# Projecting a tile's attention output in two halves instead of four quarters

## The chip, the cores and the metric

The kernel runs on one core of one Trainium2 chip. The metric is the device time of one execution in microseconds, as the median of several runs. In the texts below TensorE, VectorE, ScalarE, GpSimd and SyncE are the core's engines; the profile calls them PE (with PEld for its weight loads), DVE, ACT, POOL and SP.

## What is computed

The program is a graph network of 1250 nodes with 512 features: two graph layers and two feed-forward layers that contain attention, each added to a running sum `x`. Only the last of them, the second attention, is touched by the change:

```python
qkv = x @ qkv_w.T + qkv_b                       # x here: normalised x plus a 3-wide convolution
q, k, v = jnp.split(qkv, [c, 2 * c], axis=-1)   # 8 heads of 64
logits = jnp.einsum('bmd,bpd->bmp', qd * scale, kd)
_, idx = lax.top_k(logits, 16)                  # each query keeps its 16 best keys
...
attn = jax.nn.softmax(jnp.einsum('bmd,bmkd->bmk', q * scale, k_sel), axis=-1)
out = jnp.einsum('bmk,bmkd->bmd', attn, v_sel)
...
return out @ wo_w.T + wo_b                      # the projection that the change re-cuts
```

The result of this layer is added to `x`, and that sum is the program's output, 1250 rows by 512 columns in float32.

## The kernel before, in words

The 1250 nodes are cut into 10 tiles of 125 rows. The second attention takes 40 steps in an order that is written out by hand (`tc.manual_schedule()`): each engine executes its instructions in the order in which the program emits them. Step `n` treats tile `n // 4` and one pair of heads, `c = n % 4`; the two heads of a pair are called 0 and 1. A step does the following.

- `scores1` (L1595): TensorE multiplies the queries of the tile with all 1250 keys into one of two score buffers, which take three PSUM banks each, one for each head of a pair. The score pair `scores1(n + 1, 0, 0)`, two matmuls, is the first work of the next step and stands in the middle of the emitted order.
- `largest1`, `first1`, `second1` (L1602 to L1626): VectorE finds each row's 16 largest scores and from them `nm`, the negated maximum, and `below`, the threshold.
- `weights1` (L1632): ScalarE writes the exponentials `e`. `select1` (L1639, L1642): ScalarE writes the signs `sg` of score minus threshold, the last read of a score buffer, and GpSimd multiplies `e` by them.
- `turn1(n - 1, g)` (L1652) and `keep1(n - 1, g)` (L1659): TensorE transposes the weights of the step before in five groups of four blocks, and ScalarE copies each group to `pT`, with a Relu that drops what was not selected.
- `values1(n - 2, ...)` (L1708) and `outputs1` (L1718): TensorE multiplies the transposed weights with the values of the step before that one, and ScalarE keeps the result in `oT`, for which three buffers are there.
- Once in a tile, spread over its four steps: the sums of the exponentials (L1668 to L1693), their transposes on TensorE (L1689) at c = 2, the scaling of `oT` (L1696) on GpSimd, and `halves1` (L1580 to L1583) for the next tile's queries.
- `project1(i - 1, c)` (L1726): with `i = n // 4 - 1`, TensorE multiplies the scaled `oT` of the tile two before the current one with 128 of the 512 columns of `w_o`, as a sum of four products. Each float32 product is two instructions in the profile. `finish1` (L1734, L1736): VectorE adds `X` to it in the tile `y1`, and after the last columns of a tile SyncE writes that to the output.

The groups of transposes, the sums of values, the transposed sums and the results of `project1` all live in one pool of two PSUM banks, `ps_to1`; each new tile of that pool gets a bank when the kernel is built, and waits until the tile that had the bank before has been read.

The condition `i >= 1` leaves the first eight steps without a projection. The 32 calls in the loop serve tiles 0 to 7; tiles 8 and 9 are projected in full width behind the loop, into the score buffers.

Of the kernel before, what the change touches and what calls it, by code (L numbers as in the profile page):

```python
# [22 lines left out]
D = 512  # L23
# [549 lines left out]
def tile_usual(ctx: ExitStack, tc: tile.TileContext, a: dict, out: bass.AP):  # L573
# [165 lines left out]
    with (  # L739
# [83 lines left out]
        for r in range(rounds):  # L823
# [7 lines left out]
            while order and (order[0][0] <= r or r == rounds - 1):  # L831
                _, i, t = order.pop(0)
# [720 lines left out]
    with (  # L1553
# [17 lines left out]
        def halves1(i, a_):  # L1571
            if i >= T:
                return
            if a_ == 0:
                stacks[i] = at1.tile([128, 2, H, P], F32R, name="stacks")
            S = stacks[i]
            own, other = PAIRS[a_]
            hi, lo = S[own, 0, a_::2, :], S[own, 1, a_::2, :]
            q = qT[own, :, span(i, i + 1)]
            nc.scalar.copy(hi, q)  # L1580
            nc.gpsimd.tensor_sub(lo, q, hi.bitcast(F32))
            nc.sync.dma_start(S[other, 1, a_::2, :].bitcast(F32), hi.bitcast(F32))
            nc.sync.dma_start(S[other, 0, a_::2, :].bitcast(F32), lo.bitcast(F32))  # L1583

        def scores1(n, a_, *chunks):
            if n > last:
                return
            i, j = steps[n]
            h = 2 * j + a_
            if (n, a_) not in score:  # L1590
                score[n, a_] = ps_s1[a_].tile([P, 3 * 512], F32, name="S")
            for c in chunks:
                n0, n1 = PIECES[a_][c]
                for x in range(2):
                    nc.tensor.matmul(score[n, a_][:, n0:n1], stacks[i][:, x, h, :], K2[:, h, n0:n1],  # L1595
                                     start=(x == 0), stop=(x == 1))


        def largest1(n, a_):
            largest[n, a_] = at1.tile([P, SEARCHED, 8], F32, tag=f"largest{a_}", name="largest")  # L1600
            for k in range(SEARCHED):
                nc.vector.max(out=largest[n, a_][:, k, :], in_=score[n, a_][:, k:N:SEARCHED])  # L1602
# [32 lines left out]
        def select1(n, a_):  # L1635
            if not 0 <= n <= last:
                return
            sg = at1.tile([P, N], F16, tag=f"sg{a_}", name="sg", bufs=1)
            nc.scalar.activation(sg, score.pop((n, a_))[:, :N], AF.Sign, bias=belows.pop((n, a_)),  # L1639
                                 accum_out=signs[:, 2 * n + a_ : 2 * n + a_ + 1])  # L1640
            e = es[n, a_]
            (nc.vector if 2 * n + a_ == 2 * last + 1 else nc.gpsimd).tensor_mul(e, e, sg)  # L1642
# [27 lines left out]
        def sums_exp1(i):  # L1670
            nc.scalar.activation(sums[i], sums[i], AF.Exp)
# [23 lines left out]
        def scale1(i):  # L1695
            nc.gpsimd.tensor_mul(oTs[i], oTs[i], sums.pop(i))  # L1696

        def values1(n, t0, t1):
            if not 0 <= n <= last:
                return  # L1700
            i, j = steps[n]
            if t0 == 0:
                outs[n] = ps_to1.tile([128, 512], F32, tag="to", name="O")
            pT = pTs[n]
            for t in range(t0, t1):
                for a_ in range(2):
                    h = 2 * j + a_
                    nc.tensor.matmul(outs[n][a_ * DH : (a_ + 1) * DH, :P],  # L1708
                                     V[:, t, h * DH : (h + 1) * DH], pT[:, a_ * T + t, :],
                                     start=(t == 0), stop=(t == T - 1))  # L1710
# [9 lines left out]
        def project1(i, c, width=D // K, y=None):  # L1720

            if y is None:
                y = ps_to1.tile([128, 512], F32, tag="to", name="O")[:P, :width]
            cols = slice(c * width, (c + 1) * width)
            for k in range(K):
                nc.tensor.matmul(y, oTs[i][:, k, :], w_o[:, k, cols], start=(k == 0), stop=(k == K - 1))  # L1726
            projected.append((i, cols, y))
# [16 lines left out]
        def keep_late1():  # L1744
            if lates:
                t, ps = lates.pop(0)
                nc.vector.tensor_add(V[:, t, :], ps[:P], v_b)
# [17 lines left out]
        with tc.manual_schedule():  # L1765
            nc.sync.dma_start(w_v, a["qkv"][:, 2 * D :].rearrange("(k p) f -> p k f", p=128))
            nc.sync.dma_start(v_b, bass.AP(tensor=a["v_b"].tensor, offset=a["v_b"].offset, ap=[[0, P], [1, D]]))
            for a_ in range(2):
                halves1(0, a_)
            scores1(0, 0, 0, 2, 1)  # L1770
            for n in range(len(steps)):


                i, c = n // K - 1, n % K
                if i >= 0 and c == 3:
                    scale1(i)
                select1(n - 1, 1)
                largest1(n, 0)
                values1(n - 2, 0, 5)
                first1(n, 0)  # L1780
                if n == 1:
                    keep_late1()
                second1(n, 0)
                values1(n - 2, 5, 8)
                turn1(n - 1, 0)
                keep1(n - 1, 0)
                values1(n - 2, 8, T)
                scores1(n, 1, 1)
                scores1(n, 1, 0)
                outputs1(n - 2)  # L1790
                if i >= 0 and c == 1:
                    sums_over1(i)
                weights1(n, 0)
                if i >= 0 and c == 2:
                    sums_turn1(i)
                    sums_keep1(i)
                turn1(n - 1, 1)
                scores1(n, 1, 2)
                if n < 2:
                    values_late1(T - 3 + 2 * n)  # L1800
                keep1(n - 1, 1)
                turn1(n - 1, 2)
                if i >= 0 and c == 0:
                    sums1(i)
                if i >= 1:
                    project1(i - 1, c)
                select1(n, 0)
                largest1(n, 1)
                keep1(n - 1, 2)
                finish1()  # L1810
                if c < 2:
                    halves1(steps[n][0] + 1, c)
                if i >= 0 and c == 1:
                    sums_wide1(i)
                scores1(n + 1, 0, 0)
                if i >= 0 and c == 0:
                    sums_exp1(i)
                if n == 1:
                    keep_late1()
                turn1(n - 1, 3)  # L1820
                keep1(n - 1, 3)
                first1(n, 1)
                if n == 0:
                    keep_late1()
                scores1(n + 1, 0, 2)
                scores1(n + 1, 0, 1)
                if n == 0:
                    values_late1(T - 2)
                weights1(n, 1)
                turn1(n - 1, 4)  # L1830
                keep1(n - 1, 4)
                second1(n, 1)

            n, i = len(steps), T - 1
            sums1(i)
            values1(n - 2, 0, 5)
            select1(n - 1, 1)
            turn1(n - 1, 0)  # L1840
            values1(n - 2, 5, T)
            keep1(n - 1, 0)
            outputs1(n - 2)
            sums_exp1(i)
            turn1(n - 1, 1)
            keep1(n - 1, 1)
            sums_over1(i)
            sums_wide1(i)
            y0 = ps_s1a.tile([P, 3 * 512], F32, name="S")
            y1 = ps_s1b.tile([P, 3 * 512], F32, name="S")  # L1850
            project1(i - 1, 0, D, y0[:, :D])
            turn1(n - 1, 2)
            keep1(n - 1, 2)
            finish1()
            sums_turn1(i)
            sums_keep1(i)
            turn1(n - 1, 3)
            keep1(n - 1, 3)
            R = sums.pop(i)
            oT = oTs[i]  # L1860
            nc.vector.tensor_mul(oT[:, : K - 1, :], oT[:, : K - 1, :], R[:, : K - 1, :])  # L1861

            def terms(*ks):
                for k in ks:
                    nc.tensor.matmul(y1[:, :D], oT[:, k, :], w_o[:, k, :], start=(k == 0), stop=(k == K - 1))  # L1865

            terms(0)
            turn1(n - 1, 4)
            signs_over1()
            terms(1)  # L1870
            keep1(n - 1, 4)
            values1(n - 1, 0, T)
            terms(2)
            nc.vector.tensor_mul(oT[:, K - 1, :], outs.pop(n - 1)[:, :P], R[:, K - 1, :])
            terms(K - 1)
            projected.append((i, slice(0, D), y1[:, :D]))
            finish1()
# [62 lines left out]
```

## Time and profile before

| what | value |
| --- | --- |
| median of 3 runs | 1506.62 us (1504.06 to 1507.05) |
| the profiled execution's own time | 1506.82 us |
| its span, first to last instruction | 1504.9 us |
| mean granted TensorE clock | 0.990 |
| second attention, 1110.07 to 1496.60 us | 386.53 us: TensorE busy 373.04, ScalarE 337.05, VectorE 299.97, GpSimd 244.64 |
| matmul instructions of `project1` in the loop (L1726) | 256 of 125 x 128, median 0.273 us |
| additions in `finish1` in the loop (L1734) | 32 of 125 x 128, median 0.269 us |

All times within the profile are microseconds from the start of the span. A busy TensorE in it is not TensorE at its peak, since matmuls are pipelined and their ends are modelled. A line such as L1726 is a line of the kernel. The idle time in square brackets is the engine's idle time ahead of a group of instructions, with the engine, tile and line that ended it.

### The profile page before, as it was taken

How to read it: one execution, taken by the hardware profiler on the slowest of the kernel's cores; microseconds unless marked ns; L12 is line 12 of the kernel's file. 1: busy time of each engine (PE TensorE's matmuls, PEld its weight loads, DVE VectorE, ACT ScalarE, POOL GpSimd, SP SyncE). 2: the span in 40 equal slices, each digit the busy share in tenths (PEclk: the TensorE clock that was granted, in tenths of full speed). 3: DMA queues.
4: the chain of work that ended last, by engine and by line, in shares of the span. 5: the costliest groups of instructions: out<-in, count | busy, mean ns of one | idle time of the engine just before them, and what ended most of it. 6: DMA issues, size and time to landing. Idle time of an engine off the chain costs nothing. (4 is left out here: it accounts for less than half of the span.)

```text
span 1504.9 us, 22522 instructions
## 1 busy us (share of the span) xinstructions
PE 1424.8 (95%) x8127; PEld 936.5 (62%) x8127; DVE 830.4 (55%) x2852; ACT 707.8 (47%) x1351; POOL 350.1 (23%) x301
## 2 busy tenths in 40 slices
PE   6999999978999998999999999998988999999997
PEld 4566744457778776544544445664447788888885
DVE  8995667644444332341111263565377888887774
ACT  2334434455555553301111122432148999999984
POOL 0110000011111111000000021320026666666662
PEclk9999999989999999999999999999999999999999
DMA  4001000010101000201000000000020001001000
GB/s 141 30 0 57 1 0 1 1 47 16 43 15 49 21 24 18 63 28 56 29 28 28 28 29 29 0 29 0 5 79 15 15 22 25 22 23 25 22 9 24
DMA packets 42332, 41.19 MB, mean 27 GB/s; under 512 B 25738, under 2 KB 30084, under 8 KB 42211
## 3 DMA queue, kind: packets, MB, share of 16 engines
q1 hardware_dynamic: 42211, 39.66, 9.0%
q8 instruction: 66, 1.08, 0.3%
q14 instruction: 55, 0.45, 0.1%
HBM read 26.81 MB, written 2.56 MB: 20 GB/s over the span
## 5 line engine op out<-in xcount | busy, mean ns | idle before, releaser
L1642 POOL TENSOR_TENSOR e<-e,sg 125x1250 f32<-125x1250 f32 x79 | 203.5, 2575 | 127.0 <-ACT sg L1639 75.0
L1602 DVE MAX8 largest<-S 125x8 f32<-125x89 f32 (+1 forms) x1120 | 183.9, 241 | 51.3 <-PE S L1595 51.2
L1336 DVE SCALAR_TENSOR_TENSOR X<-ps_o,gate,X 125x512 f32<-125x512 f32 x80 | 60.0, 749 | 177.1 <-PE ps_o L1334 177.1
L1595 PE MATMUL S<-K,stacks 128*125 128x512 f32 x480 | 133.5, 389 | 14.3 <-ACT sg L1639 6.2
L1334 PE MATMUL ps_o<-we,hid 128*125 128x512 f32 x320 | 141.2, 595 | 0.0
L1659 ACT ACTIVATE pT<-ps_t 125x500 f32<-125x500 f32 x200 | 117.8, 589 | 37.7 <-PE ps_t L1652 32.7
L1652 PE MATMUL ps_t<-ident,e 125*125 125x125 f32 x800 | 132.2, 285 | 2.8 <-ACT pT L1659 1.3
L1652 PEld LDWEIGHTS ps_t<-ident,e 125*125 125x125 f32 x800 | 109.5, 187 | 35.1 <-ACT pT L1659 14.3
L1329 ACT ACTIVATE hid<-ps_mm,b 128x500 f32<-128x500 f32 (+1 forms) x40 | 24.6, 615 | 209.0 <-PE ps_mm L1326 209.0
L1326 PE MATMUL ps_mm<-yT,we 128*128 128x500 f32 (+1 forms) x320 | 115.8, 520 | 0.0
L1708 PE MATMUL O<-pT,yT 125*64 125x125 f32 x1600 | 104.7, 275 | 0.2 <-ACT pT L1659 0.2
L1632 ACT ACTIVATE e<-S,nm 125x1250 f32<-125x1250 f32 x80 | 104.4, 1305 | 0.2
L1639 ACT ACTIVATE sg<-S,below 125x1250 f16<-125x1250 f32 x80 | 104.5, 1307 | 0.0
L1334 PEld LDWEIGHTS ps_o<-we,hid 128*125 128x125 f32 x320 | 59.0, 187 | 72.4 <-issue 69.6
L1127 ACT COPY pT<-ps_t 125x500 f32<-125x500 f32 (+3 forms) x112 | 54.8, 489 | 94.3 <-PE ps_t L1122 93.3
L1326 PEld LDWEIGHTS ps_mm<-yT,we 128*128 128x128 f32 x320 | 60.3, 189 | 55.2 <-issue 53.3
L1595 PEld LDWEIGHTS S<-K,stacks 128*125 128x125 f32 x480 | 72.7, 190 | 33.8 <-ACT sg L1639 18.0
L1708 PEld LDWEIGHTS O<-pT,yT 125*64 125x64 f32 x1600 | 85.8, 136 | 10.5 <-DVE bad L1762 0.8
L1034 PE MATMUL S<-K,stacks 128*125 128x512 f32 (+10 forms) x288 | 84.3, 401 | 7.1 <-ACT e L1101 6.6
L1122 PE MATMUL ps_t<-ident,e 125*125 125x125 f32 x440 | 81.7, 296 | 9.5 <-ACT pT L1127 6.0
L640 ACT ACTIVATE rs<-rs 125x1 f32<-125x1 f32 x60 | 12.1, 203 | 162.9 <-DVE rs L639 159.5
L1005 POOL TENSOR_TENSOR stacks<-yT,stacks 64x125 fp32r<-64x125 f32 x80 | 34.3, 428 | 232.1 <-ACT stacks L1004 229.0
(241 smaller groups left out, 2534.6 us busy)
## 6 DMA issues: line engine op xcount, KB each, us to landing
we<-in_W SPq DMA_DIRECT2D x16, 512.0 KB
stacks<-stacks SPq DMA_DIRECT2D x160, 31.2 KB
stacks<-stacks SPq DMA_DIRECT2D x40, 125.0 KB
X<-in_x SPq DMA_DIRECT2D x5, 500.0 KB
out<-y SPq DMA_DIRECT2D x10, 250.0 KB
w_n<-in_wn SPq DMA_DIRECT2D x1, 1024.0 KB
w_c<-in_wc SPq DMA_DIRECT2D x1, 1024.0 KB
w_q<-in_Wq SPq DMA_DIRECT2D x1, 1024.0 KB
```

Source lines behind the costliest of these rows:

```text
L1034: nc.tensor.matmul(ps[:, n0:w], stacks[n][:, x, a_, :], K2[:, 2 * j + a_, n0:w], start=(x == 0), stop=(x == 1))
L1122: nc.tensor.transpose(ps[:P, span(t - t0, t - t0 + 1)], es[n, a_][:, span(t, t + 1)], ident[:P, :P])
L1326: nc.tensor.matmul(ps[:, :n], w1[:, k, f * 128 : (f + 1) * 128], yT[:, k, span(t0, t1)], start=(k == 0), stop=(k == K - 1))
L1334: nc.tensor.matmul(ps[:P], hid[:, f, span(t, t + 1)], w2[:, f, :], start=(f == 0), stop=(f == FF // 128 - 1))
L1595: nc.tensor.matmul(score[n, a_][:, n0:n1], stacks[i][:, x, h, :], K2[:, h, n0:n1], start=(x == 0), stop=(x == 1))
L1602: nc.vector.max(out=largest[n, a_][:, k, :], in_=score[n, a_][:, k:N:SEARCHED])
L1632: nc.scalar.activation(e, score[n, a_][:, :N], AF.Exp, bias=maxima.pop((n, a_)))
L1639: nc.scalar.activation(sg, score.pop((n, a_))[:, :N], AF.Sign, bias=belows.pop((n, a_)), accum_out=signs[:, 2 * n + a_ : 2 * n + a_ + 1])
L1642: (nc.vector if 2 * n + a_ == 2 * last + 1 else nc.gpsimd).tensor_mul(e, e, sg)
L1652: nc.tensor.transpose(turned[n, g][:P, span(b - g0, b - g0 + 1)], es[n, b // T][:, span(b % T, b % T + 1)], ident[:P, :P])
L1659: nc.scalar.activation(pTs[n][:, g0:g1, :], turned.pop((n, g))[:P, : (g1 - g0) * P].rearrange("p (t n) -> p t n", n=P), AF.Relu)
L1708: nc.tensor.matmul(outs[n][a_ * DH : (a_ + 1) * DH, :P], V[:, t, h * DH : (h + 1) * DH], pT[:, a_ * T + t, :], start=(t == 0), stop=(t == ...
```

## The change

In steps c = 0 and c = 2 of a tile nothing is projected any more. In steps c = 1 and c = 3, at the same place in the order, `project1` is called for 256 columns in place of 128: columns 0 to 255 at c = 1 and 256 to 511 at c = 3. `finish1` is unchanged in the code; it finds something to add in every second step, twice as wide, and creates `y1` at c = 1 in place of c = 0.

```diff
@@ -1802,8 +1802,8 @@
                 turn1(n - 1, 2)
                 if i >= 0 and c == 0:
                     sums1(i)
-                if i >= 1:
-                    project1(i - 1, c)
+                if i >= 1 and c % 2 == 1:
+                    project1(i - 1, c // 2, D // 2)
                 select1(n, 0)
                 largest1(n, 1)
                 keep1(n - 1, 2)
```

## The prediction

> **What bounds the kernel now.** The page comes first. TensorE is busy for 95% of the span, so the first question is whether it is really the limit in the stage that changes.
>
> ```profile
> PE 1424.8 (95%) x8127; PEld 936.5 (62%) x8127; DVE 830.4 (55%) x2852; ACT 707.8 (47%) x1351; POOL 350.1 (23%) x301
> ```
>
> The second attention runs from about 1110 us to the end. I cut it at the start of each step's score pair, the first two score matmuls of the next step (L1595 x2 in the timeline, with the one wait for ScalarE's `sg`). The diff moves work that stands right ahead of this pair. The first eight steps project nothing, because `i >= 1` is not met, so the stage holds its own control group. The view is the busy times by stretch: start and end, length, then busy time of TensorE, its weight loads, VectorE, ScalarE and GpSimd.
>
> ```profile
> 1148.14:1157.01 8.87, 7.83 (x72) 6.51 (x72) 7.16 (x45) 7.95 (x13) 5.51 (x3) 1.00 0.01 2
> 1157.01:1165.92 8.91, 7.86 (x73) 6.54 (x73) 7.66 (x47) 8.65 (x15) 6.17 (x3) 1.00 0.14 31
> 1165.92:1175.43 9.51, 8.42 (x76) 7.04 (x77) 7.21 (x45) 9.15 (x15) 7.01 (x4) 1.00 0.13 28
> 1175.43:1184.33 8.90, 7.86 (x73) 6.53 (x73) 7.12 (x45) 7.96 (x13) 6.36 (x3) 1.00 0.01 2
> 1184.33:1193.22 8.89, 8.72 (x81) 7.41 (x81) 7.16 (x45) 7.95 (x13) 5.51 (x3) 1.00 0.01 2
> 1193.22:1202.38 9.16, 9.02 (x81) 7.31 (x81) 7.65 (x48) 8.65 (x15) 6.18 (x3) 1.00 0.14 30
> 1202.38:1211.88 9.50, 9.34 (x84) 7.88 (x84) 7.30 (x46) 9.14 (x15) 6.84 (x4) 1.00 0.13 29
> 1211.88:1221.03 9.15, 9.00 (x81) 7.31 (x81) 7.22 (x46) 7.96 (x13) 6.36 (x3) 1.00 0.00 1
> ```
>
> The upper four stretches end with steps c = 0, 1, 2, 3 of a tile without a quarter; the lower four are the same c, each ending with its quarter. TensorE does 0.9 to 1.1 us more in each of the lower four, yet c = 0 and c = 2 cost nothing (8.89 against 8.87, 9.50 against 9.51), while c = 1 and c = 3 cost 0.25 (9.16 against 8.91, 9.15 against 8.90). The granted clock is 1.00 in both groups. So a quarter is hidden where it stands, and something else costs 0.25 in every second stretch. The weight-load timeline shows both (start, length, line, tile, the idle time ahead and who ended it):
>
> ```profile
> 1164.52 0.29 PEld L1652 LDWEIGHTS ps_t<-ident,e 125*125 125x125 f32 x2 [0.31 <-POOL e L1642]
> 1165.91 0.29 PEld L1595 LDWEIGHTS S<-K,stacks 128*125 128x125 f32 x2 [1.11 <-ACT sg L1639]
> ...
> 1192.00 0.95 PEld L1726 LDWEIGHTS O<-w_o,oT 128*125 128x125 f32 x8
> 1193.21 0.29 PEld L1595 LDWEIGHTS S<-K,stacks 128*125 128x125 f32 x2 [0.26 <-ACT sg L1639]
> ...
> 1195.07 0.51 PEld L1652 LDWEIGHTS ps_t<-ident,e 125*125 125x125 f32 x4 [0.43 <-ACT pT L1659]
> ...
> 1201.09 0.95 PEld L1726 LDWEIGHTS O<-w_o,oT 128*125 128x125 f32 x8
> 1202.38 0.29 PEld L1595 LDWEIGHTS S<-K,stacks 128*125 128x125 f32 x2 [0.34 <-ACT sg L1639]
> ...
> 1203.85 0.64 PEld L1652 LDWEIGHTS ps_t<-ident,e 125*125 125x125 f32 x4
> ```
>
> First, the score pair waits for `sg` (`select1(n, 0)`, which frees the score banks): 1.11 us without a quarter, 0.26 to 0.34 with one. A quarter fills a wait. Second, after the quarters of c = 0 and c = 2 the fifth group of transposes (`turn1(n - 1, 4)`, at 1195.07) waits 0.43 us for ScalarE to drain the group just before it: these tiles share two banks with the quarter, and as the kernel is built the fifth group got the fourth's bank, not the quarter's. After c = 1 and c = 3 (1203.85) there is no such wait, nor in steps without a quarter. That is the 0.25. The chain of waits runs, in each step, from the score pair through TensorE (transposes, scores, value sums, scores, transposes) to ScalarE's `pT` and `sg` and back to the pair; the quarters are not on it.
>
> **The change part by part.** *Even steps (c = 0, 2) lose their quarter.* The pair still starts with `sg`, so the time under the quarter becomes waiting: gain 0 there. The bank pressure goes too. I take the stretch behind to become that of the steps without a quarter: 9.16 to 8.91 and 9.15 to 8.90. Bounds: 0 if the build still gives the fifth group the fourth's bank, 0.25 if not; I take 0.25, because the list of waits from 1139 to 1192 us, where no quarter runs, has no transpose waiting for `pT` at all, and that from 1193 to 1476 has 47.
>
> *Odd steps (c = 1, 3) get twice the columns:* the same four products (eight instructions) with 256 columns. No row shows 256. The nearest:
>
> ```profile
> 1192.11 1.04 PE L1726 MATMUL O<-w_o,oT 128*125 128x128 f32 x8
> 1193.22 0.72 PE L1595 MATMUL S<-K,stacks 128*125 128x512 f32 x2
> ...
> 1483.90 3.60 PE L1726 MATMUL S<-w_o,oT 128*125 128x512 f32 x8
> ```
>
> One of 128 columns lasts 0.273 by its line's median, so eight in 1.04 start (1.04 - 0.273) / 7 = 0.110 apart; at 512 columns (0.592 each) it is (3.60 - 0.592) / 7 = 0.430. Those are the ends for 256 columns: 0.110 and 0.430. Both are near 0.85 ns a column, so the row between is read off the line: 0.110 + 0.320 x 128 / 384 = 0.217. Eight take 1.73, against 0.88 for a quarter.
>
> The Trainium skill speaks for the change here: "TensorE: Matmul & The Clock Gate", section Back-to-back issue gap, gives sustained spacings of about 81 ns at 128 columns and 131 at 512, so an estimate of 98 at 256 and 0.78 for eight. The rows here (110 and 430, each product in two instructions) disagree; by the page the half would fit under the wait, and the sum would be that of the third rival.
>
> The room: the first quarter's matmuls start at 1192.11 and the pair starts with `sg` at 1193.22, which is 1.11. This stretch follows one without a quarter, as every odd step will. The half then ends 1.73 - 1.11 = 0.62 after `sg`, and the pair starts 0.62 late. With the ends it is 0 (8 x 0.110 fits) and 2.33.
>
> Who waits: queued behind the half on TensorE are the pair, the fourth transposes, the scores and all of the chain named above. ScalarE's `pT` of the fourth group waits for TensorE today (0.79 and 0.16 idle at c = 3 and c = 1 by its timeline), so nothing on ScalarE absorbs the delay, and I carry 0.62 in full.
>
> *VectorE:* per tile four additions of 0.270 become two; by the rows at 128 (0.270) and 512 columns (0.686) one of 256 takes 0.41, so 1.08 becomes 0.82. VectorE waits for scores in these stretches, so this is nothing on the path. The addition stands ahead of `first1(n, 1)` and now starts when the half ends: that `nm` comes about 0.7 late, while its reader, the exponential on ScalarE, moves 0.62 late and had 0.7 to spare. Cost 0; without that margin it would be about 0.1 a time. The output DMA leaves SP in the same step as before, after 0.9 us more of TensorE: hidden, as nobody waits for it before the end.
>
> *Sum per tile:* before 9.16 + 9.50 + 9.15 + 8.89 = 36.70; after 8.87 + (8.91 + 0.62) + 9.51 + (8.90 + 0.62) = 37.43. That is +0.73, in eight tiles (32 quarters by four) +5.8. The profiled execution lasted 1506.82 (span 1504.9), 0.2 above the median 1506.62; put on the median it is 1512.4.
>
> **The rivals.** *The bank wait moves to the odd steps.* There a product still stands between the third and fourth transposes, and the first quarter of all, behind steps without one, is one that has the wait (1195.07). Against it: the half delays the fourth group by 0.62 while VectorE's release moves less. Price 0.25 x 16 = 4.0 more: +9.8, 1516.4.
>
> *The even steps keep the wait.* Then the odd step's room is that of 1201.09 to 1202.38: with the first matmul 0.1 behind its load, 1.19, delay 0.54, 1.08 a tile, +8.6: 1515.2. The control group speaks against it.
>
> *Faster: the half fits.* If 256 columns cost little more per instruction than 128, the pair is not late, and only the bank wait goes: 36.70 to 36.19 a tile, -4.1: 1502.5. The place is the pair at the end of odd steps. It breaks even at a delay of 0.26, so at (1.11 + 0.26) / 8 = 0.171 per instruction; below that the change is faster, above slower. For it: the pair does wait today. Against it: 0.217 by two rows on one line.
>
> *About no change:* a delay near 0.26, from a spacing between 0.15 and 0.19 or a ScalarE queue that absorbs part: 1506.6.
>
> **How the numbers follow.** Forecast 0.58, wait in the odd steps 0.20, wait kept 0.06, faster 0.07, no change 0.09. What a measurement can tell here is 0.2%, about 3 us. Slower by more than that: 0.58 + 0.20 + 0.06 = 0.84. The range takes in the forecast and the two slower rivals, with 1.6 above the highest for the spread of the runs (1504.06 to 1507.05), and reaches down to 1508.5, a delay of about 0.38: 0.84 of the chance or a little less.
>
> **What would show it.** In the profile after: 128 matmuls of 256 columns at L1726, spaced 0.21 to 0.22; stretches of about 8.87, 9.53, 9.51, 9.52; the pair behind a half without a wait for `sg`, and behind an even step with about 1.1 of it; no wait of the fifth transposes for `pT` after even steps. A spacing under 0.17, or a pair that still waits for `sg` behind a half, would prove it wrong; fifth transposes that wait 0.43 after odd steps would show the first rival.

## The result, and the profile after

The changed kernel takes 1509.01 us (1507.76 to 1511.63, 12 runs) against 1505.66 us (1504.06 to 1507.05, 12 runs): a ratio of 1.0024, 95% interval 1.0015 to 1.0033. It is 3.4 us slower, where 5.8 was forecast. (As a time, 1512.4 was forecast; 1.0 us of the distance to 1509.01 lies in the time before, which is 1505.66 over 12 runs and was 1506.62 over three.) Its profiled execution lasted 1508.96 us, with a span of 1507.0.

The spans differ by only 2.1, because the two profiled executions also differ ahead of the change: the score pair behind the first c = 0 step that may project starts at 1193.22 before and at 1191.82 after. The comparison is therefore made inside the loop, from this pair to the start of the last projection: 1193.22 to 1476.64 is 283.42 before, 1191.82 to 1478.90 is 287.08 after, so +3.66; from there to the end of the second attention it is 0.13 less. That is +3.5, the size of what the runs show.

The view by stretch of the changed kernel, from one score pair to the next, with the columns of the table shown before (length, then TensorE, weight loads, VectorE, ScalarE, GpSimd, and last the granted clock, the DMA share and GB/s); they end with c = 1, 2, 3, 0:

```profile
1191.82:1201.18 9.36, 9.23 (x80) 7.90 (x81) 8.02 (x50) 9.08 (x16) 6.62 (x4) 1.00 0.15 31
1201.18:1210.76 9.58, 8.50 (x78) 7.10 (x76) 7.08 (x43) 8.71 (x14) 6.40 (x4) 1.00 0.13 28
1210.76:1220.06 9.30, 9.21 (x80) 7.89 (x81) 7.54 (x48) 8.37 (x13) 6.75 (x4) 1.00 0.00 1
1220.06:1229.03 8.97, 7.93 (x75) 6.58 (x73) 7.07 (x44) 7.53 (x13) 5.11 (x3) 1.00 0.10 30
```

Their sum is 37.21 a tile, against 36.70 before and 37.43 in the prediction. TensorE does the same products, the granted clock is still 1.00, but it now idles in the even steps. The weight loads show where:

```profile
1191.82 0.29 PEld L1595 LDWEIGHTS S<-K,stacks 128*125 128x125 f32 x2 [1.13 <-ACT sg L1639]
...
1193.29 0.64 PEld L1652 LDWEIGHTS ps_t<-ident,e 125*125 125x125 f32 x4
...
1199.53 1.59 PEld L1726 LDWEIGHTS O<-w_o,oT 128*125 128x125 f32 x8
1201.15 0.40 PEld L1595 LDWEIGHTS S<-K,stacks 128*125 128x125 f32 x2
...
1202.73 0.64 PEld L1652 LDWEIGHTS ps_t<-ident,e 125*125 125x125 f32 x4
```

The pair behind an even step waits for `sg`: 1.13 us in these rows (c = 0), 1.26 behind c = 2. Behind a half (1201.15) nobody is waited for: `sg` is done and the pair is late. The fifth transposes (1193.29, 1202.73) wait for nothing, behind even or odd steps. The matmuls of one half and of the pair behind it, and the line's summary (shortest, median and longest duration in ns):

```profile
1199.64 1.89 PE L1726 MATMUL O<-w_o,oT 128*125 128x256 f32 x8
1201.18 0.82 PE L1595 MATMUL S<-K,stacks 128*125 128x512 f32 x2
1201.84 0.60 PE L1652 MATMUL ps_t<-ident,e 125*125 125x125 f32 x4
```

```profile
L1726 PE MATMUL O<-w_o,oT x128: 377/379/382, 1199.6 to 1480.4; 128*125 128x256 f32 x128
```

The spacing of 256 columns is (1.89 - 0.379) / 7 = 0.216, so a half takes 1.73.

One caution on reading stretches: a pair that need not wait is recorded 0.07 to 0.1 early: its record starts at 1201.18, only 0.03 after that of the half's last instruction (1199.64 + 7 x 0.216 = 1201.15), though the instructions of the half are 0.216 apart. Part of a late pair's delay therefore appears in the stretch behind it (9.58 and 8.97, where a pair that waits gives 9.51 and 8.89). Stretches are best added by twos.

### The profile page after: what moved, and what is told of

It reads as the page before. It is cut to its first block, busy times and chain, and to the rows that moved or that the text cites. A ratio compares the mean times of both kernels' runs of the same rounds, so it can differ in the third digit from the quotient of the medians.

```text
span 1507.0 us, 22250 instructions
## 1 busy us (share of the span) xinstructions
PE 1411.8 (94%) x7999; PEld 930.9 (62%) x7999; DVE 831.4 (55%) x2836; ACT 707.1 (47%) x1351; POOL 350.1 (23%) x301
## 5 line engine op out<-in xcount | busy, mean ns | idle before, releaser
L1652 PEld LDWEIGHTS ps_t<-ident,e 125*125 125x125 f32 x800 | 113.4, 187 | 30.3 <-POOL e L1642 8.4
L1708 PE MATMUL O<-pT,yT 125*64 125x125 f32 x1600 | 104.7, 275 | 0.0
L1708 PEld LDWEIGHTS O<-pT,yT 125*64 125x64 f32 x1600 | 85.8, 136 | 10.2 <-DVE bad L1762 0.8
```

Of the source, the lines that this page charges most:

```text
L1652: nc.tensor.transpose(turned[n, g][:P, span(b - g0, b - g0 + 1)], es[n, b // T][:, span(b % T, b % T + 1)], ident[:P, :P])
L1708: nc.tensor.matmul(outs[n][a_ * DH : (a_ + 1) * DH, :P], V[:, t, h * DH : (h + 1) * DH], pT[:, a_ * T + t, :], start=(t == 0), stop=(t == ...
```

## The experiments

The theory after the result: the even steps gain 0.25 each because the fifth transposes no longer wait for the bank, and the odd steps lose about 0.5 because the product is longer than the wait for `sg`. In all four runs the shared pool's banks are assigned by hand. The first starts from the kernel before, the other three from the changed kernel, in which no transpose of the loop waits for `pT` as it is, so that the assignment alone has nothing to remove there. The added lines:

```diff
+        def bank1(name, other=True):
+            turns[0] += other
+            return ps_to1.tile([128, 512], F32, tag=f"to{turns[0] % 2}", name=name, bufs=1)
...
-            turned[n, g] = ps_to1.tile([128, 512], F32, tag="to", name="ps_t1")
+            turned[n, g] = bank1("ps_t1")
```

and likewise for the pool's other tiles. In these files the added lines move the later ones by 3, or by 4: the score pair is L1598, the transposes are L1655, the projection is L1729 or L1730.

**Quarters, with the banks strictly in turn.** Only the lines above are added to the kernel before.

> The kernel before with its four quarters, but the tiles of the shared pool take the two banks strictly in turn, so that the fifth transposes always get the bank of the quarter and never that of the fourth transposes. Theory (the even steps' gain in the changed kernel is the bank wait alone): the stretches become about 8.9, 8.9, 9.5, 8.9 us with all quarters in place, 36.2 a tile against 36.7, and the kernel takes about 4.0 us less than before, 1501.7 against 1505.7. Rival (the gain comes from TensorE having less to do in even steps, the bank is by the way): the stretches stay at 9.16 and 9.15 behind c = 0 and c = 2 and the time stays at 1505.7.

Measured: 1503.68 us (9 runs) against 1506.74 (23 runs), ratio 0.9979, interval 0.9969 to 0.9988. The stretches, ending with c = 0, 1, 2, 3, all with their quarter:

```profile
1187.03:1195.91 8.88, 8.71 (x81) 7.40 (x81) 7.16 (x45) 7.95 (x13) 5.51 (x3) 1.00 0.01 2
1195.91:1204.82 8.91, 8.75 (x81) 7.33 (x81) 7.65 (x48) 8.65 (x15) 6.18 (x3) 1.00 0.14 31
1204.82:1214.33 9.51, 9.35 (x85) 7.89 (x85) 7.31 (x47) 9.15 (x15) 6.84 (x4) 1.00 0.13 29
1214.33:1223.22 8.89, 8.72 (x81) 7.32 (x81) 7.21 (x46) 7.95 (x13) 6.36 (x3) 1.00 0.00 1
```

and its weight loads around the end of c = 0:

```profile
1194.69 0.95 PEld L1729 LDWEIGHTS O<-w_o,oT 128*125 128x125 f32 x8
1195.91 0.29 PEld L1598 LDWEIGHTS S<-K,stacks 128*125 128x125 f32 x2 [0.26 <-ACT sg L1642]
...
1197.38 0.63 PEld L1655 LDWEIGHTS ps_t<-ident,e 125*125 125x125 f32 x4
```

The quarter and its short wait for `sg` are as before (0.26), the 0.43 ahead of the fifth transposes is gone, and the tile takes 36.19, which is exactly what the four stretches without any projection took (8.87 + 8.91 + 9.51 + 8.90). The rival falls: with all of TensorE's work in place the 0.25 go, so they were the bank. Of the forecast 4.0 the runs show 3.1, with 4.0 inside the interval. This kernel computes the whole result and is faster than both, by 0.2% against the kernel before.

**Half as many products in a half.**

```diff
-            for k in range(K):
-                nc.tensor.matmul(..., start=(k == 0), stop=(k == K - 1))
+            for k in range(ks):      # ks = 2 in the loop; K behind it
+                nc.tensor.matmul(..., start=(k == 0), stop=(k == ks - 1))
```

> The changed kernel (banks strictly in turn) with the last two of the four products of each half left out, so the projection of tiles 0 to 7 lacks half of its sum; the 256-column result and its 256-column addition stay. Four instructions of 256 columns take 4 x 0.216 = 0.86 us, as long as a quarter. Theory (the loss is the pair that starts late behind a product longer than the wait for sg): the pair waits for sg again, stretches 8.9, 8.9, 9.5, 8.9, time 1501.7, about 7 below the changed kernel. Rival (the loss is the wider addition or the later release by VectorE): the stretches stay at 9.4, 9.6, 9.3, 9.0 and the time at 1509.

Measured: 1502.76 us against 1506.74, ratio 0.9973 (0.9963 to 0.9983); stretches 8.90, 9.51, 8.87, 8.89, ending with c = 1, 2, 3, 0. The weight loads of the products and of the pair behind them:

```profile
1199.69 0.73 PEld L1730 LDWEIGHTS O<-w_o,oT 128*125 128x125 f32 x4
1200.87 0.29 PEld L1598 LDWEIGHTS S<-K,stacks 128*125 128x125 f32 x2 [0.45 <-ACT sg L1642]
```

The pair waits for `sg` again and the whole loss is gone, although the result and its addition are still 256 columns wide. The loss is thus in the length of the product; the width of the addition costs nothing. The addition also starts earlier here than behind the whole half, so this run does not speak about its lateness; the part on VectorE below does.

**Three of four products,** `ks = 3`.

> As the run with two products, but with three of four (the last one left out, so the projection of tiles 0 to 7 lacks a quarter of its sum): six instructions, 6 x 0.216 = 1.30 us. By the prediction's sum the room is 1.11, the pair is 0.19 late, the stretches with a half are 9.10 and 9.09 and the time is 1501.7 + 15 x 0.19 = 1504.5. By the theory that a pair that does not wait for sg also has its weight load of about 0.1 hidden behind the product, the room is 1.22, the pair 0.08 late, the stretches 8.99 and 8.98 and the time 1502.9.

Measured: 1503.44 us against 1506.74, ratio 0.9979 (0.9971 to 0.9988). The run's time cannot tell 1502.9 from 1504.5; its stretches can. They end with c = 1, 2, 3, 0:

```profile
1193.69:1202.63 8.94, 8.80 (x78) 7.52 (x79) 7.59 (x47) 8.69 (x15) 6.21 (x4) 1.00 0.16 32
1202.63:1212.22 9.59, 8.50 (x79) 7.10 (x77) 7.40 (x47) 9.11 (x15) 6.83 (x4) 1.00 0.13 28
1212.22:1221.11 8.89, 8.79 (x78) 7.48 (x79) 7.11 (x45) 7.95 (x13) 6.37 (x3) 1.00 0.00 1
1221.11:1230.08 8.97, 7.93 (x74) 6.59 (x73) 7.39 (x46) 7.95 (x13) 5.51 (x3) 1.00 0.10 30
```

By twos these are 18.53 and 17.86; with all quarters and no bank wait they are 18.42 (8.91 + 9.51) and 17.78 (8.89 + 8.89). One shortened half costs 0.11 and 0.08, where the prediction's room says 0.19 and the theory of the hidden load 0.08. The full half costs 18.94 - 18.42 = 0.52 and 18.27 - 17.78 = 0.49. From three products (6 x 0.216 = 1.30) the room is 1.30 - 0.10 = 1.20, from four (1.73) it is 1.73 - 0.50 = 1.23. Two points, one room of about 1.2, and beyond it the delay grows nearly as the product: 0.43 more of it gave 0.41 more delay in both stretches.

**The bank wait put behind the halves.**

```diff
-            turned[n, g] = bank1("ps_t1")
+            turned[n, g] = bank1("ps_t1", not (g == 4 and shared[0]))   # shared[0]: this step has a half
```

> The changed kernel, whole, with the bank wait of the prediction's first rival put in by hand: behind a half the fifth transposes get the bank of the fourth, elsewhere the banks are taken in turn. If that wait costs behind a half what it cost behind a quarter, the stretches behind halves (those that end with c = 2 and c = 0) grow by 0.25 to about 9.83 and 9.22, and the time is 1509.0 + 15 x 0.25 = 1512.8. If the later fourth transposes leave room for it, nothing changes: 1509.0.

Measured: 1514.26 us against 1506.74, ratio 1.0048 (1.0035 to 1.0061), 0.24% more than the changed kernel's. The fifth transposes behind a half:

```profile
1222.11 0.51 PEld L1655 LDWEIGHTS ps_t<-ident,e 125*125 125x125 f32 x4 [0.43 <-ACT pT L1662]
```

```profile
1201.14:1210.86 9.72, 8.63 (x79) 6.88 (x77) 7.09 (x44) 8.72 (x14) 6.40 (x4) 1.00 0.13 28
...
1220.18:1229.40 9.22, 8.02 (x75) 6.50 (x73) 7.06 (x44) 7.53 (x12) 5.10 (x3) 1.00 0.10 30
```

The wait is back, and the stretch that ends with c = 0 grows by the expected 0.25 (8.97 to 9.22), but the one that ends with c = 2 only by 0.14 (9.58 to 9.72). The trace shows where the other half went: into the first 32 instructions of the value sums, in the changed kernel (L1708) and in this run (L1711).

```profile
1203.49 2.07 PE L1708 MATMUL O<-pT,yT 125*64 125x125 f32 x32
```

```profile
1203.71 1.94 PE L1711 MATMUL O<-pT,yT 125*64 125x125 f32 x32
```

In the steps c = 0, 1 and 3 of both kernels they take 1.94. So at this place the changed kernel has a pause of 0.13, which is gone in this run: that much of the delay falls into a pause that was there anyway. In the last tile the changed kernel takes 1.94 there too, without the pause, and the same stretch grows by 0.23 (9.46 to 9.69). What the pause waits for was not tried and stays open. The sum over the loop, 7 x 0.14 + 0.23 + 7 x 0.25 = 3.0, is less than the 3.8 expected; the ratios give 0.0024 x 1506 = 3.6 and cannot separate the two.

## Why the prediction was right, and which term was off

- **What bounds the stage.** Right. A quarter fills a wait for `sg`; taking it out of even steps gained nothing there. The pair behind them waits 1.13 and 1.26, where 1.11 was read from a step without a quarter.
- **The bank wait.** Right in place and size: no transpose behind an even step waits for `pT` in the changed kernel, and the run with quarters and alternating banks shows that the 0.25 was the bank's. That the build would give the fifth transposes the quarter's bank behind a half too was put down as the likelier of two cases, by a weighing and not by following the build, and came true: here the prediction had some luck; the first rival's mechanism, put in by hand, costs about what was priced at c = 0 and half of that at c = 2. The prediction's count of 47 waits of transposes for `pT` says less than it seems: 16 are those of the fifth transposes, 0.43 each. The other 31 are waits of 0.18 to 0.19 of the fourth, which the run with alternating banks still has, at 36.19 a tile.
- **The spacing.** Right: 0.217 was read off the line between 128 and 512 columns, 0.216 measured. The rival in which the half fits needed less than 0.171 and falls. The estimate of 98 ns worked out from the Trainium skill ("TensorE: Matmul & The Clock Gate", section Back-to-back issue gap) does not hold for these products, which took 216.
- **The delay of the pair: the mis-sized term.** 0.62 was forecast, 0.50 measured, because the room is 1.2 and not 1.11. The room was taken up to the record of a pair that waits for `sg`. Such a pair still has its weight load ahead of it in full, about 0.1 us; a pair that comes late has loaded its weights behind the product. From the record of a pair that waited to the fourth transposes it is 0.56 to 0.58 (before, 1193.22 to 1193.78). Behind a half the product has run its length at 1199.64 + 1.73 = 1201.37, and the fourth transposes start at 1201.84, only 0.47 later. The difference is about 0.1. The run with three products confirms the room; that the 0.1 is the load is read from the rows, not tried by itself. The other reading, that the pair is 0.62 late and ScalarE takes up a part of it, does not fit: then the next copy that waits for TensorE, that of the fourth group to `pT`, would be 0.62 late. From the last record of `sg` to this copy it is 2.01 in the changed kernel and 1.47 in the run with quarters and alternating banks, a delay of 0.54, where the stretches show 0.52. The rows of both, at c = 1:

```profile
1200.46 0.20 ACT L1639 ACTIVATION_READ_ACCUMULATOR sg<-S,below 125x1 f32 x1
...
1202.47 0.59 ACT L1659 ACTIVATE pT<-ps_t 125x500 f32<-125x500 f32 x1 [0.69 <-PE ps_t L1652]
```

```profile
1204.56 0.20 ACT L1642 ACTIVATION_READ_ACCUMULATOR sg<-S,below 125x1 f32 x1
...
1206.03 0.59 ACT L1662 ACTIVATE pT<-ps_t 125x500 f32<-125x500 f32 x1 [0.15 <-PE ps_t L1655]
```

- **The number of delays.** The prediction took 16. The last half, in step 39, has no score pair behind it: before, the fourth transposes there idle 0.62 for `pT` behind the quarter, after, the half covers that. From the projection's start to the end it is 19.96 before and 19.83 after. The row before:

```profile
1478.40 1.14 PE L1652 MATMUL ps_t<-ident,e 125*125 125x125 f32 x8 [0.62 <-ACT pT L1659]
```

- **The sum, made again.** 8 x (0.52 + 0.49) less one of 0.49 is 7.6, less 16 x 0.25 = 4.0 for the bank, is +3.6, beside +3.5 in the loop and the tail, and 3.4 by the runs. From the forecast 5.8, the smaller delay takes 16 x (0.62 - 0.505) = 1.8 and the missing sixteenth delay 0.5.
- **VectorE and the output.** Right: the addition measures 0.422 (0.41 forecast), VectorE waits about 0.25 for the half, and the run with two products shows no cost from its width. Nor does its lateness cost anything: the 0.54 are there at the copy above, which waits for TensorE, and the whole stretch grows by no more. The addition behind the half at 1199.64:

```profile
1201.57 0.42 DVE L1734 TENSOR_TENSOR y<-X,O 125x256 f32<-125x256 f32 x1 [0.25 <-PE O L1726]
```

## What to carry to other kernels

Here work in the shadow of a wait was free up to 1.2 us and cost nearly its full length beyond. So cut such work to the shadow, and spread it over as many shadows as there are, before joining pieces to save instructions. When equal pieces of work cost something in every second step only, look at the buffers they share: here the remedy was the order of two banks, not the size of the piece. Measure the room to where the waiting instruction starts its real work, not to where its record starts.

## What the runs showed of the hardware that was not expected

The room under the wait was 1.2 us by two runs, where the records gave 1.11. The rows fit a matmul that starts its work about 0.1 us sooner behind another one, with its weights loaded, than after a wait; that the load is the cause was not tried by itself. One instruction of the projection costs 0.110, 0.216 and 0.430 us at 128, 256 and 512 columns, nearly in proportion to the columns, so wider pieces of it save nothing on TensorE. That does not go for every product that the profile calls f32: the two instructions of the score pair, 512 columns each, whose operands the kernel declares F32R, take 0.72 together (at 1193.22 before), where two of the projection's would take 0.430 + 0.592 = 1.02.
